# g and h formed with the positions on the partitions, g's statistics as plain sums, and the next pair's squarings beside the first batch's entry

## The chip, the cores and the metric

The kernel runs on one core of a Trainium2 chip, in float32 throughout except for packed sign weights. The metric is device microseconds of one execution. A core has TensorE (PE, matrix products into PSUM), VectorE (DVE), ScalarE (ACT), GpSimd (POOL) and SyncE (SP, which here only issues DMAs); each runs its own queue, and they wait for one another by semaphores.

## The reference, cut to what matters

Four blocks follow one another on x of 8 x 512 x 32 x 32, that is 8 batches of 512 channels and 1024 positions. The change touches only the first:

```
f = relu(batchnorm(Wf x + bf))        # 64 channels; statistics over all batches and positions
g = relu(batchnorm(Wg x + bg))        # 64 channels, the same
h = Wh x + bh                         # 64 channels
z = f^T g                             # 1024 x 1024 for each batch
z2 = (z / largest singular value of z) applied to h
x = Wv z2 + bv + x
```

The second block normalises x over groups of 16 channels and applies an attention over 1024 positions (wq, wk, wv, wp); the third is an attention of its own; the fourth multiplies the signs of x with the signs of a weight matrix. They are done batch by batch in the main loop.

## The kernel before, in words

**First block without z.** z is never formed. The largest singular value comes from the 64 x 64 Gram matrices f f^T and g g^T (their product has the squared singular values of z as eigenvalues), and h g^T gives what h needs. Two batches make a pair: their 64-channel rows stand side by side on the 128 partitions and in the 128 columns of a Gram product, so there are four pairs.

**First stage** (L1229 to L1274). For each batch, x (four chunks of 128 channels by 1024 positions) is the moving operand and the weights of f, g or h are stationary. Each of f, g and h is a PSUM bank: 64 channels of the first 512 positions on the lower partitions, those of the last 512 on the upper. f and g are copied to SBUF (L1261, L1264) and their statistics taken by BN_STATS (L1262, L1265), channels on the partitions. h is biased (L1269), and in the next batch turned by four TensorE transposes (`turn`, L1131) into a tile with the positions on the partitions, one tile for each pair (`ht_pair`). Loads of x go round two buffers on SP's queue, so the load for batch b waits until batch b - 2 is used up; other weights are loaded behind them. In between come the signs of the last block's weights (b = 3, 5) and, in the last batch ahead of h, the turning of wq (`natural`, L1201).

**Statistics** (L1368 to L1398). The batch statistics are gathered, summed over the two partition halves with a product against `fold`, and made into a scale and a bias for each channel; ScalarE then applies scale, bias and relu to f and g in one instruction per batch (`relu`, L1361) and f is stored to DRAM for later.

**Squarings of the last pair** (L1447 to L1456). `turned_pair` (L1347) turns f and g by eight transposes each and `gram` (L1332) forms a Gram matrix by eight products. `chain` (L1009) multiplies the two Gram matrices and then squares the result 20 times, with a rescaling by its trace at every third one; at the end a logarithm of the traces gives the singular value. The batches 6 and 7 go first (their x is still in SBUF), so the last pair's chain runs in a stretch where TensorE's order is the order of the code (`tc.manual_schedule`); between two squarings stand steps of `filler` (L1418): products of weights with weights, then Gram matrices of the other three pairs (`grams`, L1355), with a relu of another batch at each step. Outside that stretch, and on the other engines everywhere, a planner sets each engine's order by readiness and code order with a cost model.

**Entry of the first batch** (`entering`, L859, `enter`, L401). In the same written order come seven steps: the products of the batch's weights, four visits (one for each 128 channels: products of f with the weights, added into x on VectorE with L420, statistics by L423), and two steps of group statistics. The remaining filler steps stand between them: 2, 3, 3, 3, 3, 4, 6 (L1457).

**Main loop** (`fast`, L878). For each of the eight batches come the two attentions and the last block. The products with seven instead of eight terms (`seven`, L332; products by L387) fill most of it. The chains of the other three pairs (`behind`, L1122) run here: `chore` (L887) makes one squaring at every second step while there are any; a chain has 22 steps, 21 of them with a squaring.

Of the kernel before, what the change touches and what calls it, by code (L numbers as in the profile page):

```python
# [8 lines left out]
F32 = mybir.dt.float32  # L9
F16 = mybir.dt.float16  # L10
I32 = mybir.dt.int32
AF = mybir.ActivationFunctionType
# [73 lines left out]
def kernel(  # L86
# [58 lines left out]
    def side(i):  # L145

        return slice(i * MID, (i + 1) * MID)
# [14 lines left out]
    fg = sbw["fg"] = a1.tile([P, CC, P], F32, tag="fg", name="fg")  # L162
    for cc in range(CC):
        nc.scalar.dma_start(out=fg[:, cc, :], in_=w_fg[:, cc, :])
    first = load_x(0, True)
    load_w("h", w_h, [P, CC, MID], a1, nc.scalar)
# [27 lines left out]
    nc.gpsimd.memset(ones1, 1.0)  # L194

# [5 lines left out]
    bhc = const.tile([P, 1], F32, tag="bhc", name="bhc")  # L201
    wv2 = const.tile([P, C], F32, tag="wv2", name="wv2")
    for i in range(2):
        nc.gpsimd.dma_start(out=bhc[side(i), :], in_=rows[0:MID].rearrange("(p o) -> p o", o=1))
# [922 lines left out]
    fs, gs = ([a1.tile([P, HF], F32, tag=f"{n}{b}", name=f"{n}{b}") for b in range(B)] for n in "fg")  # L1127
    ht_pair = [a1.tile([P, NT, P], F32, tag=f"ht{j}", name=f"ht{j}") for j in range(NPAIR)]
    st = a1.tile([P, 2, B, 6], F32, tag="st", name="st")
# [97 lines left out]
    w0 = [sbw["fg"][:, :, 0:MID], sbw["fg"][:, :, MID:], sbw["h"]]  # L1227
    last = None
    for b in range(B):  # L1229
# [7 lines left out]
        banks = [bank() for _ in w0]  # L1237

        def products(i, cc):
            for h in range(NH):  # L1240
                mm(  # L1241
                    out=banks[i][side(h), :],
                    lhsT=w0[i][:, cc, :],
                    rhs=xt[:, cc, half(h)],
                    start=cc == 0,
                    stop=cc == CC - 1,
                )

        if b == 0:
            for cc in range(CC):  # L1250
                for i in range(2):
                    products(i, cc)
        for i in range(3):
            if b == B - 1 and i == 2:
                for _ in natural("q", "w3"):
                    pass
            if b or i == 2:
                for cc in range(CC):
                    products(i, cc)
            if i == 0:  # L1260
                nc.scalar.copy(fs[b], banks[i])  # L1261
                nc.vector.bn_stats(st[:, 0, b, :], fs[b])  # L1262
            elif i == 1:
                nc.vector.tensor_copy(gs[b], banks[i])  # L1264
                nc.vector.bn_stats(st[:, 1, b, :], gs[b])  # L1265
                if last is not None:
                    turn(last[0], last[1], ht_pair[last[0] // 2], 0)
        hraw = a2.tile([P, HF], F32, tag="hraw", name="hraw")
        nc.scalar.activation(hraw, banks[2], AF.Identity, bias=bhc)  # L1269
        last = b, hraw  # L1270
        if b == 3:
            total3 = sign_weights()
        if b == 5:
            scale_signs(total3)  # L1274

# [71 lines left out]
    def turned_pair(j):  # L1347
        ft = a2.tile([P, NT, P], F32, tag="ft", name="ft")
        gt = a2.tile([P, NT, P], F32, tag="gt", name="gt")
        for src, dst in ((fs, ft), (gs, gt)):  # L1350
            for i in range(2):
                turn(2 * j + i, src[2 * j + i], dst, i)
            yield ft, gt
# [7 lines left out]
    def relu(b, i):  # L1361
        t = (fs, gs)[i][b]
        nc.scalar.activation(t, t, AF.Relu, bias=bi0[:, i : i + 1], scale=sc0[:, i : i + 1])
        if i == 0:
            nc.sync.dma_start(out=f_dram[b], in_=t)


    mv = a1.tile([P, 2, 2], F32, tag="mv", name="mv")  # L1368
    mean = a1.tile([P, 2], F32, tag="mean", name="mean")
    dev = a1.tile([P, 2], F32, tag="dev", name="dev")  # L1370
    for i in range(2):
        nc.vector.bn_aggr(mv[:, i, :], st[:, i, :, :])
    nat_k = natural("k", "q")
    next(nat_k)
    turn(last[0], last[1], ht_pair[last[0] // 2], 0)
    ps = bank()
    mm(out=ps[:, 0:2], lhsT=fold, rhs=mv[:, :, 0], start=True, stop=True)
    nc.vector.tensor_copy(mean, ps[:, 0:2])
    nc.vector.tensor_tensor(dev, mv[:, :, 0], mean, ALU.subtract)
    nc.vector.tensor_tensor(dev, dev, dev, ALU.mult)  # L1380
    nc.vector.tensor_tensor(dev, dev, mv[:, :, 1], ALU.add)
    ps = bank()
    mm(out=ps[:, 0:2], lhsT=fold, rhs=dev, start=True, stop=True)
    sc0 = rsqrt_eps(a1, ps[:, 0:2], 2, "r0")
    bi0 = a1.tile([P, 2], F32, tag="bi0", name="bi0")
    m0 = a1.tile([P, 2], F32, tag="m0", name="m0")
    c0 = COL["L0_conv_bf"]
    bias, gamma, beta = (ct[:, c0 + 2 * i : c0 + 2 * i + 2] for i in range(3))
    nc.vector.tensor_tensor(sc0, sc0, gamma, ALU.mult)
    nc.vector.tensor_tensor(m0, mean, bias, ALU.add)  # L1390
    nc.vector.tensor_tensor(bi0, bias, m0, ALU.subtract)
    nc.vector.tensor_tensor(bi0, bi0, sc0, ALU.mult)
    nc.vector.tensor_tensor(bi0, bi0, beta, ALU.add)
    jl = order[0] // 2
    for i in range(2):
        for k in range(2):
            relu(2 * jl + k, i)
# [49 lines left out]
    relus = iter([(2 * j + k, i) for j in rest for i in range(2) for k in range(2)])  # L1447
    with tc.manual_schedule(engines={mybir.EngineType.PE}):
        steps = entering(0)
        for k, _ in enumerate(chain(jl, True)):  # L1450
# [3 lines left out]
            for args in (next(relus, None),):  # L1454
                if args:
                    relu(*args)  # L1456
        for n in (2, 3, 3, 3, 3, 4, 6):  # L1457
            next(steps)
            for _ in range(n):
                next(todo, None)  # L1460
        for _ in todo:
            pass
# [193 lines left out]
```

## Time and profile before

| | us |
|---|---|
| median of 3 runs | 1911.45 (1911.01 to 1911.63) |
| the profiled execution | 1911.79 |
| its span | 1909.9 |
| PE busy | 1886.4 |
| DVE busy | 1130.2 |
| ACT busy | 510.3 |
| first stage, until the last product of h | 4.6 to 98.1 |
| statistics, first Gram matrices | 98.1 to 114.0 |
| squarings of the last pair | 114.0 to 162.6 |
| entry of the first batch, to the first product on differences | 162.6 to 195.1 |
| main loop | 195.1 to the end |

The profile is of one execution. In a chain of waits each line has a start and a length in us, the engine, the tile written and the line of the code. In lines that list instructions, "x48" is the number of records; a float32 product leaves two records. In windows of busy time each engine's figure is the us in which it worked.

### The profile page before, as it was taken

How to read it: one execution, taken by the hardware profiler on the slowest of the kernel's cores; microseconds unless marked ns; L12 is line 12 of the kernel's file. 1: busy time of each engine (PE TensorE's matmuls, PEld its weight loads, DVE VectorE, ACT ScalarE, POOL GpSimd, SP SyncE). 2: the span in 40 equal slices, each digit the busy share in tenths (PEclk: the TensorE clock that was granted, in tenths of full speed). 3: DMA queues.
4: the chain of work that ended last, by engine and by line, in shares of the span. 5: the costliest groups of instructions: out<-in, count | busy, mean ns of one | idle time of the engine just before them, and what ended most of it. 6: DMA issues, size and time to landing. Idle time of an engine off the chain costs nothing.

```text
span 1909.9 us, 16334 instructions
## 1 busy us (share of the span) xinstructions
PE 1886.4 (99%) x6118; PEld 977.5 (51%) x6118; DVE 1130.2 (59%) x1762; ACT 510.3 (27%) x811; POOL 224.5 (12%) x176
## 2 busy tenths in 40 slices
PE   9999999999999999999999999999999999999997
PEld 4366456544745447444645446544645455544653
DVE  3256676448664677447664676457753775466547
ACT  2142121134212332035202431034202521234014
POOL 0000011201121011200121011201120011101121
PEclk9999999999999999999999999999999999999999
DMA  8420000002000120002000120002000200010001
GB/s 320 159 78 6 0 6 12 1 12 88 17 1 0 34 72 12 1 11 88 17 1 0 38 68 12 0 13 87 11 1 9 91 12 0 1 34 22 12 0 46
DMA packets 27782, 66.45 MB, mean 35 GB/s; under 512 B 4272, under 2 KB 5424, under 8 KB 27056
## 3 DMA queue, kind: packets, MB, share of 16 engines
q1 hardware_dynamic: 26768, 64.90, 10.1%
q8 instruction: 50, 0.82, 0.2%
q10 hardware_dynamic: 864, 0.43, 0.1%
q14 instruction: 36, 0.29, 0.1%
q0 software_dynamic: 64, 0.00, 0.0%
HBM read 38.51 MB, written 18.87 MB: 30 GB/s over the span
## 4 chain that ended last, share of the span: by engine, by line
PE 92%; DVE 7%; issue 1%; ACT 1%; DMA 0%; POOL 0%; DVEq 0%; ACTq 0%
PE bank L387 42%; PE bank L556 20%; PE bank L951 6%; PE bank L805 6%; PE bank L1241 5%; PE bank L657 3%; PE bank L411 2%; PE bank L674 2%; DVE both L748 1%; DVE both L718 1%; PE wide L1281 1%; PE wide L1335 1%; PE bank L1022 1%; PE bank L1023 1%; PE bank L697 1%; PE bank L826 1%
## 5 line engine op out<-in xcount | busy, mean ns | idle before, releaser
L556 PE MATMUL bank<-e,vt 128*128 128x512 f32 x768 | 334.2, 593 | 0.0
L556 PEld LDWEIGHTS bank<-e,vt 128*128 128x128 f32 x768 | 144.9, 190 | 174.8 <-issue 173.2
L387 PE MATMUL bank<-ut,h 128*128 128x512 f32 x384 | 182.3, 597 | 0.0
L344 DVE TENSOR_TENSOR e<-bank,e 128x512 f32<-128x512 f32 x128 | 87.8, 686 | 81.9 <-PE bank L387 80.8
L387 PE MATMUL bank<-us,hs 128*128 128x512 f32 x256 | 121.5, 597 | 1.3 <-DVE us L316 0.5
L387 PEld LDWEIGHTS bank<-ut,h 128*128 128x128 f32 x384 | 71.4, 190 | 95.6 <-issue 84.0
L951 PE MATMUL bank<-e,tpg 128*128 128x512 f32 x256 | 114.7, 595 | 0.0
L805 PE MATMUL bank<-tpg 128*128 128x512 f32 x256 | 114.6, 592 | 0.0
L812 ACT ACTIVATE e<-bank 128x512 f32<-128x512 f32 x128 | 76.4, 597 | 128.6 <-PE bank L805 128.6
L387 PE MATMUL bank<-h,wu 128*128 128x512 f32 x192 | 90.4, 593 | 2.4 <-DVE h L462 1.7
L387 PE MATMUL bank<-wo,h 128*128 128x256 f32 x384 | 91.8, 382 | 0.0
L817 DVE TENSOR_TENSOR esum<-esum,e 128x1024 f32<-128x1024 f32 x48 | 58.8, 1225 | 54.9 <-ACT e L812 54.9
L359 POOL TENSOR_TENSOR e<-e 128x512 f32<-128x512 f32 x32 | 43.4, 1356 | 403.8 <-ACT e L338 238.3
L951 PEld LDWEIGHTS bank<-e,tpg 128*128 128x128 f32 x256 | 48.1, 190 | 63.2 <-issue 63.1
L805 PEld LDWEIGHTS bank<-tpg 128*128 128x128 f32 x256 | 48.6, 190 | 60.7 <-issue 60.5
L387 PEld LDWEIGHTS bank<-wo,h 128*128 128x128 f32 x384 | 71.6, 190 | 13.5 <-ACT vt L338 4.1
L359 POOL TENSOR_TENSOR ut<-ut 128x512 f32<-128x512 f32 x16 | 21.7, 1359 | 476.1 <-ACT ut L340 476.1
L344 DVE TENSOR_TENSOR vt<-bank,vt 128x512 f32<-128x512 f32 x64 | 44.1, 689 | 56.2 <-PE bank L387 55.8
L387 PEld LDWEIGHTS bank<-us,hs 128*128 128x128 f32 x256 | 47.1, 190 | 54.9 <-issue 48.3
L834 DVE RECIPROCAL rsum<-bank 128x512 f32<-128x512 f32 x15 | 50.4, 3358 | 38.2 <-PE bank L826 38.2
L685 ACT ACTIVATE sg<-xt,rb 128x512 f16<-128x512 f32 x64 | 45.0, 718 | 103.7 <-DVE xt L676 100.2
L1241 PE MATMUL bank<-xt,fg 128*64 128x512 f32 x256 | 59.5, 613 | 4.6 <-DMA fg<-in_w_fg 4.6
(330 smaller groups left out, 3017.2 us busy)
## 6 DMA issues: line engine op xcount, KB each, us to landing
xt<-in_x SPq DMA_DIRECT2D x55, 512.0 KB
out<-both SPq DMA_DIRECT2D x63, 256.0 KB
rfull<-rsum SPq DMA_DIRECT2D x60, 128.0 KB
f_dram<-f SPq DMA_DIRECT2D x8, 256.0 KB
fb<-f_dram SPq DMA_DIRECT2D x8, 256.0 KB
w<-in_w SPq DMA_DIRECT2D x1, 1024.0 KB
q<-in_w_q SPq DMA_DIRECT2D x1, 1024.0 KB
k<-in_w_k SPq DMA_DIRECT2D x1, 1024.0 KB
```

The source lines that it names most:

```text
L344: nc.vector.tensor_tensor(dst, ps, u, ALU.add)
L359: nc.gpsimd.tensor_tensor(c22, c22, c12, ALU.add)
L387: mm(out=ps[:, q * w : (q + 1) * w], lhsT=lt(ka, kb, q, k), rhs=rhs(ka, kb, q, k), start=first and q == 0 and k == 0, stop=last and k == 1 ...
L556: mm(out=ps, lhsT=a[:, t, bass.ts(r_, P)], rhs=e[t], start=first and t == 0, stop=last and t == NTH - 1, skip_group_check=True,)
L657: mm(out=ps[:, i, :], lhsT=xt[:, cc, bass.ts(4 * h + i, P)], rhs=sbw["tpg"][:, cc, 2 * P : 3 * P], start=cc == 0, stop=cc == CC - 1,)
L685: nc.scalar.activation(sg[:, cc, :], xt[:, cc, half(h)], AF.Sign, bias=rb3[:, cc : cc + 1])
L805: mm(out=ps, lhsT=pt[:, 0, bass.ts(t, P)], rhs=tt[:, 0, half(h)], start=True, stop=True,)
L812: nc.scalar.activation(e[:, half(h)], ps, AF.Exp, scale=float(P) ** -0.5)
L817: nc.vector.tensor_tensor(esum, esum, e, ALU.add)
L834: nc.vector.reciprocal(r, ps)
L951: mm(out=banks[h], lhsT=gt[:, t, :], rhs=es[t][:, half(h)], start=t == 0, stop=t == NT - 1,)
L1241: mm(out=banks[i][side(h), :], lhsT=w0[i][:, cc, :], rhs=xt[:, cc, half(h)], start=cc == 0, stop=cc == CC - 1,)
```

## The change

f is formed as before, but after g and h. For g and h the roles are exchanged: 128 positions of x are the stationary operand and the 128 columns of both weights together the moving one, 8 groups of positions x 4 chunks for each batch, so both leave PSUM with the positions on the partitions and are written straight into the pairs' tiles. g then needs no transposes, nor h. g's channels are now in the free direction, so its statistics are sums over positions: VectorE adds g and its square over the 8 groups, and a product against 1/(B N) adds over the partitions. From g a pilot is taken off first (the mean of batch 0), so that the variance as a difference of sums stays accurate. Scale and bias of g are rows now: they are spread over the partitions by two products with the identity, and applied by two VectorE operations and a relu for each half of a pair (`relu_g`). In batch 0 the products follow the chunks as they arrive. `natural("q", ...)` comes after the last batch. `turned_pair` turns f alone. In the entry of the first batch, the filler steps become 2, 2, 2, 2, 2, 3, 4 and behind the first three of each stands one step of the next pair's chain, 16 of its 22 in all.

```diff
-    fg = sbw["fg"] = a1.tile([P, CC, P], F32, tag="fg", name="fg")
-    for cc in range(CC):
-        nc.scalar.dma_start(out=fg[:, cc, :], in_=w_fg[:, cc, :])
+    wf = a1.tile([P, CC, MID], F32, tag="wf", name="wf")
+    wgh = a1.tile([P, CC, 2, MID], F32, tag="wgh", name="wgh")
+    for cs in (slice(0, 1), slice(1, CC)):
+        nc.scalar.dma_start(out=wf[:, cs, :], in_=w_fg[:, cs, 0:MID])
+        nc.scalar.dma_start(out=wgh[:, cs, 0, :], in_=w_fg[:, cs, MID:])
+        nc.scalar.dma_start(out=wgh[:, cs, 1, :], in_=w_h[:, cs, :])
     first = load_x(0, True)
-    load_w("h", w_h, [P, CC, MID], a1, nc.scalar)
...
+    mean_of = a1.tile([P, P], F32, tag="mean_of", name="mean_of")
+    nc.gpsimd.memset(mean_of, 1.0 / (B * N))
...
-    for i in range(2):
-        nc.gpsimd.dma_start(out=bhc[side(i), :], in_=rows[0:MID].rearrange("(p o) -> p o", o=1))
+    nc.gpsimd.dma_start(out=bh_row, in_=rows[0:MID].partition_broadcast(P))
...
+    def add_up(b, g, dst):
+        sq = a2.tile([P, NT, MID], F32, tag="sq", name="sq")
+        nc.scalar.activation(sq, g, AF.Square)
+        for i, t in enumerate((g, sq)):
+            nc.vector.tensor_reduce(dst[:, i, :], t.rearrange("p t c -> p c t"), AX.X, ALU.add)
+        if b:
+            nc.vector.tensor_tensor(acc, acc, one, ALU.add)
...
+        psf, psg = bank(), wide().rearrange("p (t i c) -> p t i c", i=2, c=MID)
...
+        def products_gh(t, cc):
+            mm(
+                out=psg[:, t, :, :].rearrange("p i c -> p (i c)"),
+                lhsT=xt[:, cc, bass.ts(t, P)],
+                rhs=wgh[:, cc, :, :].rearrange("p i c -> p (i c)"),
+                start=cc == 0 and t % 4 == 0,
+                stop=cc == CC - 1,
+                skip_group_check=True,
+            )
...
         if b == 0:
             for cc in range(CC):
-                for i in range(2):
-                    products(i, cc)
...
+                products_f(cc)
+                for t in range(NT):
+                    products_gh(t, cc)
+        else:
+            for t in range(NT):
                 for cc in range(CC):
-                    products(i, cc)
...
+                    products_gh(t, cc)
+            for cc in range(CC):
+                products_f(cc)
+        g, h = (t[b // 2][:, :, side(b % 2)] for t in (gt_pair, ht_pair))
+        if b == 0:
+            nc.scalar.copy(g, psg[:, :, 0, :])
+            nc.vector.tensor_reduce(pilot, g.rearrange("p t c -> p c t"), AX.X, ALU.add)
+            ps = bank()
+            mm(out=ps[:, 0:MID], lhsT=mean_of, rhs=pilot, start=True, stop=True)
+            nc.vector.tensor_scalar(pilot, ps[:, 0:MID], float(B), None, ALU.mult)
+            nc.vector.tensor_tensor(g, g, over(pilot), ALU.subtract)
+        else:
+            nc.vector.tensor_tensor(g, psg[:, :, 0, :], over(pilot), ALU.subtract)
+        nc.vector.tensor_tensor(h, psg[:, :, 1, :], over(bh_row), ALU.add)
+        add_up(b, g, one if b else acc)
+        nc.scalar.copy(fs[b], psf)
+        nc.vector.bn_stats(st[:, b, :], fs[b])
...
+    for _ in natural("q", "w3"):
+        pass
...
     def turned_pair(j):
         ft = a2.tile([P, NT, P], F32, tag="ft", name="ft")
-        gt = a2.tile([P, NT, P], F32, tag="gt", name="gt")
-        for src, dst in ((fs, ft), (gs, gt)):
-            for i in range(2):
-                turn(2 * j + i, src[2 * j + i], dst, i)
-            yield ft, gt
+        for i in range(2):
+            turn(2 * j + i, fs[2 * j + i], ft, i)
+        yield ft, gt_pair[j]
...
+    def relu_g(j, i):
+        t = gt_pair[j][:, bass.ts(i, NT // 2), :]
+        for k, op in enumerate((ALU.mult, ALU.add)):
+            row = rows_g[:, k].rearrange("p i c -> p (i c)").unsqueeze(1)
+            nc.vector.tensor_tensor(t, t, row.to_broadcast([P, NT // 2, P]), op)
+        nc.scalar.activation(t, t, AF.Relu)
...
+    cols_g = a1.tile([P, 2, P], F32, tag="cols_g", name="cols_g")
+    rows_g = a1.tile([P, 2, 2, MID], F32, tag="rows_g", name="rows_g")
+    ps = bank()
+    for i, t in enumerate((sc0, bi0)):
+        nc.vector.tensor_copy(cols_g[:, i, :], t[:, 1:2].to_broadcast([P, P]))
+        mm(out=ps[:, side(i)], lhsT=cols_g[:, i, :], rhs=ident[:, 0:MID], start=True, stop=True)
...
-        for n in (2, 3, 3, 3, 3, 4, 6):
+        for n in (2, 2, 2, 2, 2, 3, 4):
             next(steps)
-            for _ in range(n):
+            for i in range(n):
                 next(todo, None)
+                if i < 3:
+                    next(behind)
```

## The prediction

> **What bounds the kernel now.** I read the page first, then the chain of waits in order of time from 0 to 310 us, then stretches of it. The page gives the span and the two engines that matter.
>
> ```profile
> span 1909.9 us, 16334 instructions
> PE 1886.4 (99%) x6118; PEld 977.5 (51%) x6118; DVE 1130.2 (59%) x1762; ACT 510.3 (27%) x811; POOL 224.5 (12%) x176
> ```
>
> TensorE is the bound, so a saving has to be TensorE time, or one of its few waits. Chain, first stage (start us, us, what):
>
> ```profile
> 25.43 10.45 PE bank L1241 x48
> 35.88 0.59 PE quad L1135 x4
> 36.47 10.45 PE bank L1241 x48
> 46.92 0.59 PE quad L1135 x4
> ```
>
> A batch takes 46.92 - 35.88 = 11.04 us, with no wait: 24 products of 64 columns, two column halves at once (each product leaves two records), then four transposes of h. The chain of the squarings:
>
> ```profile
> 138.14 0.89 PE wide L1335 x8
> 139.04 0.22 PE bank L1022 x2
> 139.26 0.22 PE bank L1023 x2
> 139.48 1.79 PE wide L1335 x16
> ```
>
> 128-column products with new weights each time go at 1.79/16 = 0.112 us a record, 0.22 a product. One squaring is two: 0.44 us. Here too TensorE is full (the Gram products are filler). The entry of the first batch:
>
> ```profile
> 173.74 1.06 PE bank L411 x4
> 174.80 2.77 PE wide L1281 x6
> 177.57 1.11 PE bank L411 x4
> 178.68 0.74 DVE xt L420
> 179.45 0.70 DVE st L423
> ...
> 182.41 3.54 PE wide L1281 x8
> ...
> 188.90 3.73 DVE h L462 x8
> 192.63 1.15 DVE hs L326
> 193.80 1.24 DVE hs L327
> 195.08 1.13 PE bank L387 x2
> ```
>
> Up to 178.7 a visit takes 1.06 + 2.77 = 3.83 us of TensorE against some 3.05 of VectorE; then VectorE sets the end, and TensorE waits 3.3 us (1.7, 0.7, 0.9 before L387). In the main loop one VectorE instruction per batch marks the period:
>
> ```profile
> 314.63 1.22 DVE L329 TENSOR_TENSOR hs<-h,hs 128x1024 f32<-128x1024 f32 x1
> 536.88 1.21 DVE L329 TENSOR_TENSOR hs<-h,hs 128x1024 f32<-128x1024 f32 x1
> 757.25 1.22 DVE L329 TENSOR_TENSOR hs<-h,hs 128x1024 f32<-128x1024 f32 x1
> 967.64 1.22 DVE L329 TENSOR_TENSOR hs<-h,hs 128x1024 f32<-128x1024 f32 x1
> 1176.40 1.22 DVE L329 TENSOR_TENSOR hs<-h,hs 128x1024 f32<-128x1024 f32 x1
> ```
>
> Periods 222.3, 220.4, 210.4, 208.8. The first two hold 22 squarings of the other pairs each, the later ones none; against their mean of 209.6, a squaring costs (12.7 + 10.8)/44 = 0.53 us of the main loop.
>
> **The Trainium skill.** "TensorEngine Tiling (Array Packing)", Key Properties: changing the tiling mode drains TensorE. The trace agrees: around the four transposes the two changes cost some 0.2 us (0.59, less three gaps of 0.109 between transposes and one more). "VectorE: DVE Perf Modes", tier table and errata: fp32 two-input operations and reductions run at one element a cycle, (N+151)/0.96 ns, 0.69 us for 512. The trace has 0.68 for L1413 (512) and 0.28 for the reductions of 128 (0.29 by the formula); a 512-element TENSOR_REDUCE it doesn't have, so 0.69 is an estimate, and that the strided view costs no more is my choice (0.69 to 1.4). "TensorE: Matmul & The Clock Gate", Part 1: the first microseconds run at half clock; the trace has weight loads 0.85 us apart up to 9.5 us and 0.43 after.
>
> **The change, part by part.**
>
> *First stage, batches 1 to 7.* Per batch: f by four chunks x 0.87 (four records of 0.2177) = 3.48; g and h by 32 products x 2 records x 0.112 = 7.15; two mode changes 0.2; transposes of h gone. 10.81 (10.8 to 10.9) against 11.04: 7 x 0.23 = **-1.6**. *Batch 0* interleaves both forms per chunk, eight changes instead of none: 3.48 + 7.15 + 0.8 = 11.4 against 10.45: **+1.1** (0.5 to 2; the half clock until 9.5 us costs both alike). The weights become six DMAs on ACT's queue instead of five, in 256-byte pieces; they queue behind nothing but one another, ct one issue (0.45 us) later, and it is needed for nothing early. The pilot's product waits for a copy and a reduction, 0.6 + 0.7; batch 1's products stand ready to cover it. Uncovered it costs 1.7. VectorE per batch: two subtractions/additions, two reductions, bn_stats at 0.69 each and a 0.2 sum, 3.7 us, one Square of 0.6 on ACT: hidden in 10.8 us. x must now be whole at a batch's start; x of the next batch is asked for one batch ahead, and DMA falls nearly idle for some 2 us in most batches (12 GB/s at 28 to 30 us), so hidden; a late x would cost up to 2.6 a batch.
>
> Queues: POOL's gets one broadcast of the bias of h in place of two loads and one memset more, SP's gets nothing new (x and weights are asked for in the same order, the stores of f also), so no load is passed by another; I cost this at nothing.
>
> *Statistics to the first Gram.* The transposition of the last h goes (0.50), natural q follows instead of preceding. Six extra small VectorE operations and two turns through TensorE (1.5 us) come in, but relu of f (1.52 on ACT) covers most of the latter. Before, g's two relus (1.42), transposes (0.66) and the Gram of f precede the Gram of g, 5.98 us after the first relu. Now g takes 1.5 + four VectorE operations x 0.69 + an f eviction 0.69 + the last relu 0.6, some 5.5 us, half of the Gram starting before: **-1.0** (-3 to +1).
>
> *Squarings of the last pair.* The same 38 filler steps run; three g-transposition steps (0.9 us each) become three Gram halves (0.9) drawn forward from the entry: no change on TensorE. VectorE takes 12 extra operations, 8.3 us, less three evictions, 2.1. In 114 to 130 us VectorE is busy 5.93 of 16, so most is hidden; in 130 to 144 it is busy 13.69 of 14, and a pair's four (2.8 us, less 0.7 to 1.4) fall there: **+1.3** (0.3 to 4).
>
> *Entry.* 16 squarings come in: 16 x 0.44 + five trace sums x 0.14 = 7.8; three Gram halves left: -2.7. In order: weights step +0.7; visits 1.06 + 2 x 0.86 + 2 x 0.44 = 3.7, as before; mean step 3 x 0.86 + 3 x 0.44 + 0.14 = 4.0 against 3.54, +0.5; last step inside TensorE's old 3.3 us of waiting. TensorE's order is written out, so a squaring holds up everything behind it until the one before is evicted. By ACT that takes 0.37 plus handing over, 0.65, under the 0.86 of filler: no stall. Every third squaring goes through sum, reciprocal and scaling on VectorE: 1.25 us in the main loop (product's end to eviction). There are five. VectorE's queue is in order, and a visit's own 3.05 us may stand ahead. Stalls: weights step 0.5, second visit 0.4 to 1.9 (take 1.1), third 0 to 1 (0.5), mean step 0.5; last step 0 to 1.5 of VectorE's path (0.7). Sum 0.7 + 0.5 + 3.3 = **+4.5** (+2 to +9).
>
> *Main loop.* 16 of 63 squarings leave: 16 x 0.53 = **-8.5** (7.0 by TensorE's bare time, to 9). Without TensorE being full there it would be nothing, but it is busy 209.28 of 209.40 us.
>
> Sum: -1.6 + 1.1 - 1.0 + 1.3 + 4.5 - 8.5 = -4.2. The profiled execution took 1911.79 (span 1909.9 and 1.9 around it), 0.3 above the median of 1911.45. So 1907.6 on its own time, **1907.3** against the median.
>
> **Rivals.** (a) *The squarings are only moved.* TensorE was full in the entry up to 178.7, so the 7.8 us come back whole, with somewhat larger stalls: entry +6.5, sum -2.2, 1909.3. For it: written order. Against it: 3.3 us of waits at the end.
> (b) *The entry hides them.* VectorE slips the small operations between a visit's instructions: stalls gone, entry +1.5, sum -7.2, 1904.3. For it: 0.7 us of VectorE free per visit before; against it: three dependent operations in a row.
> (c) *Slower.* VectorE runs a visit's 3.05 us ahead of every sum-and-scale: each of the five then stalls TensorE 3.05 + 1.25 - 0.86 = 3.4 us, 17 instead of my 3.3 (1.1 + 0.5 + 0.5 + 0.5 + 0.7): +9.5, 1921. It ends slower by 0.2% once the five average over (3.3 + 8.0)/5 = 2.3 us. Against it: only two or three fall inside a visit.
>
> **Chances.** 0.2%, about what a measurement of this kernel can tell from no change, is 3.8 us: below 1907.6 is faster. Forecast (-2.5 to -6.5) 0.52, of which 0.35 beyond -3.8; (a) (-2.5 to +2) 0.20; (b) (-6.5 and below) 0.16; (c) and its milder forms (above +2) 0.12, 0.10 of it beyond +3.8. Faster 0.51, same 0.39, slower 0.10. Range 1902.5 to 1913.5: it leaves out the worst of (c) and the best of (b) and reaches the ends of the entry's cost. The forecast's own: 1905 to 1909.
>
> **What would show it.** In the chain of the changed kernel: batches 1 to 7 some 10.8 us apart and batch 0 ending about 1 us later than before; the first squaring of the last pair 1 to 2 us before 114.0; from it to the first product on the differences (195.1) some 86 us where there were 81.0, with waits of TensorE for squarings' evictions of about 3 us in the entry; the first period marked by L329 still some 222, with its 22 squarings, and the second about 212 instead of 220.4, since only some 6 squarings are left for it. I would be wrong if those waits pass 6 us in all, if batch 0 or the pilot leaves TensorE idle for over 2 us, if a batch waits for x, or if the main loop gives back less than 7 us.

## The result, and the profile after

The changed kernel takes 1920.56 us (median of 5 runs, 1919.56 to 1921.56) against 1911.01 (5 runs, 1910.23 to 1911.63): a ratio of 1.0051, interval 1.004 to 1.0062. It is slower by 0.5%. I had predicted 1907.3, and my range ended at 1913.5, so both the time and its sign were wrong. The profiled execution took 1919.56 us, 1.0 below this median, and the one of before 0.8 above its own: the profiles differ by 7.8 us where the medians differ by 9.55.

The page after, first two lines:

```profile
span 1917.7 us, 16784 instructions
PE 1886.4 (98%) x6320; PEld 1007.7 (53%) x6320; DVE 1152.1 (60%) x1796; ACT 507.1 (26%) x808; POOL 224.4 (12%) x176
```

TensorE is busy for the same 1886.4 us as before, so the 7.8 us of longer span are time in which TensorE stands still: 31.3 us instead of 23.5. That is the balance of the whole execution; stage by stage its work moves too, out of the main loop and into the entry.

The timeline of TensorE in the changed kernel (start us, us, line, operands, count, and in brackets the wait ahead of it), first stage:

```profile
4.20 2.52 PE L1262 MATMUL bank<-xt,wf 128*64 128x512 f32 x4 [4.20 <-DMA wf<-in_w_fg]
7.43 3.75 PE L1271 MATMUL wide<-wgh,xt 128*128 128x128 f32 x16 [0.70 <-DMA wgh<-in_w_h]
...
27.96 3.65 PE L1262 MATMUL bank<-xt,wf 128*64 128x512 f32 x16
31.55 7.41 PE L1271 MATMUL wide<-wgh,xt 128*128 128x128 f32 x64
38.89 3.65 PE L1262 MATMUL bank<-xt,wf 128*64 128x512 f32 x16
...
111.27 2.05 PE L1371 MATMUL wide<-ft 128*128 128x128 f32 x16 [1.14 <-ACT ft L1151]
116.31 0.49 PE L1026 MATMUL bank<-gm 128*128 128x128 f32 x2 [0.56 <-DVE gm L1380]
...
118.00 0.35 PE L1058 MATMUL bank<-tj,mask 128*128 128x1 f32 x2 [0.98 <-DVE tj L1054]
```

A batch takes 38.89 - 27.96 = 10.93 us (11.04 before). Batch 0 first waits 0.70 us for the weights of h, and its 16 records of g and h take 3.75 us at the low clock (the clock records give full speed from 11.12 us on), where the next 16 take 2.05. The first squaring starts at 116.31, where it was at 114.03.

The same view, entry of the first batch. L415 are the products of a visit, L1317 filler, L1026 and L1058 a squaring and its trace, L391 the first product of the main loop:

```profile
174.88 1.13 PE L415 MATMUL bank<-fb,pv 64*128 64x512 f32 x4
...
177.49 1.10 PE L1317 MATMUL wide<-p,nat_v 128*128 128x512 f32 x2
179.60 0.49 PE L1026 MATMUL bank<-cur 128*128 128x128 f32 x2 [1.01 <-DVE cur L1048]
180.24 1.13 PE L415 MATMUL bank<-fb,pv 64*128 64x512 f32 x4
...
184.83 0.38 PE L1058 MATMUL bank<-tj,mask 128*128 128x1 f32 x2 [0.65 <-DVE tj L1054]
185.14 1.13 PE L415 MATMUL bank<-fb,pv 64*128 64x512 f32 x4
...
201.97 1.98 PE L391 MATMUL bank<-h,wu 128*128 128x512 f32 x4 [0.81 <-DVE h L466]
```

The four visits start 3.87, 5.36 and 4.90 us apart; before it was 3.90, 3.83 and 3.83. A squaring waits 1.01 us for its rescaled operand. The main loop's first product, at 189.58 before, starts at 201.97.

VectorE in the main loop, the instruction that marks the periods (L333 now, L329 before):

```profile
208.55 1.22 DVE L333 TENSOR_TENSOR hs<-h,hs 128x1024 f32<-128x1024 f32 x1
328.42 1.22 DVE L333 TENSOR_TENSOR hs<-h,hs 128x1024 f32<-128x1024 f32 x1
550.93 1.22 DVE L333 TENSOR_TENSOR hs<-h,hs 128x1024 f32<-128x1024 f32 x1
765.56 1.22 DVE L333 TENSOR_TENSOR hs<-h,hs 128x1024 f32<-128x1024 f32 x1
975.58 1.22 DVE L333 TENSOR_TENSOR hs<-h,hs 128x1024 f32<-128x1024 f32 x1
```

The periods are 119.9, 222.5, 214.6 and 210.0 us, with 18, 22, 7 and no squarings. Before they were 118.6, 222.2, 220.4 and 210.4, with 19, 22, 22 and none. So the third period gained 5.8 us and the first lost 1.3.

Cut at marks that both traces have, the 7.8 us of span lie as follows (us; "to the main loop" runs from the last of the 21 squarings to the first L333 or L329):

| stretch | predicted | measured | where it is read |
|---|---|---|---|
| the eight batches | -0.5 | +1.7 | start of what follows their products, 96.3 (98.05 without the 1.75 of wq) to 98.0 |
| from there to the first squaring, wq counted in both | -1.0 | +0.6 | 17.7 to 18.3 |
| chain of the last pair | +1.3 | +1.3 | 42.28 to 43.55 |
| entry, to the main loop | +4.5 | +8.9 | 39.78 to 48.69 |
| main loop to the end | -8.5 | -4.7 | 1713.86 to 1709.19 |
| sum | -4.2 | +7.8 | |

Two rows carry 8.2 of the 12.0 us between prediction and result: the entry and the main loop, the two ends of the 16 moved squarings.

### The profile page after: what moved, and what is told of

The parts are those of the page before. It is cut to its first block, busy times and chain, and to the rows that moved or that the text cites. A ratio compares the mean times of both kernels' runs of the same rounds, so it can differ in the third digit from the quotient of the medians.

```text
span 1917.7 us, 16784 instructions
## 1 busy us (share of the span) xinstructions
PE 1886.4 (98%) x6320; PEld 1007.7 (53%) x6320; DVE 1152.1 (60%) x1796; ACT 507.1 (26%) x808; POOL 224.4 (12%) x176
## 4 chain that ended last, share of the span: by engine, by line
PE 59%; DVE 4%; issue 0%; ACT 0%; DVEq 0%; ACTq 0%
PE bank L391 29%; PE bank L560 15%; PE bank L955 4%; PE bank L809 4%; PE bank L661 2%; PE bank L678 1%; PE bank L415 1%; DVE both L722 1%; DVE both L752 1%; PE bank L701 1%; PE bank L830 1%; DVE xt L680 0%; DVE both L714 0%; DVE us L320 0%; DVE us L317 0%
## 5 line engine op out<-in xcount | busy, mean ns | idle before, releaser
L391 PE MATMUL bank<-ut,h 128*128 128x512 f32 x384 | 182.4, 597 | 0.7 <-ACT e L353 0.7
L391 PE MATMUL bank<-us,hs 128*128 128x512 f32 x256 | 121.5, 597 | 1.3 <-DVE us L320 0.5
L391 PEld LDWEIGHTS bank<-ut,h 128*128 128x128 f32 x384 | 71.4, 190 | 96.7 <-issue 85.2
L391 PE MATMUL bank<-wo,h 128*128 128x256 f32 x384 | 91.9, 382 | 0.0
L391 PE MATMUL bank<-h,wu 128*128 128x512 f32 x192 | 90.5, 593 | 1.5 <-DVE h L466 0.8
L391 PEld LDWEIGHTS bank<-wo,h 128*128 128x128 f32 x384 | 71.7, 190 | 14.3 <-ACT vt L342 4.9
L391 PEld LDWEIGHTS bank<-us,hs 128*128 128x128 f32 x256 | 47.3, 190 | 56.4 <-issue 49.5
L1271 PEld LDWEIGHTS wide<-wgh,xt 128*128 128x128 f32 x512 | 59.6, 196 | 8.8 <-issue 8.8
```

Source lines behind the costliest of these rows:

```text
L391: mm(out=ps[:, q * w : (q + 1) * w], lhsT=lt(ka, kb, q, k), rhs=rhs(ka, kb, q, k), start=first and q == 0 and k == 0, stop=last and k == 1 ...
L1271: mm(out=psg[:, t, :, :].rearrange("p i c -> p (i c)"), lhsT=xt[:, cc, bass.ts(t, P)], rhs=wgh[:, cc, :, :].rearrange("p i c -> p (i c)"), ...
```

## The experiments

**The two halves of the change.** Theory A says that the squarings carry the loss; its rival says that the new form of g and h does. The first run leaves the squarings where they were, in the changed kernel:

```diff
             for i in range(n):
                 next(todo, None)
-                if i < 3:
-                    next(behind)
```

> The changed kernel without the squarings in the entry (filler steps 2, 2, 2, 2, 2, 3, 4 kept, all 63 squarings of the other pairs back in the main loop). Theory A (the squarings written into the entry are what made it slower): last squaring of the last pair to first VectorE instruction L333 on the differences falls from 48.7 us to 36 to 38 (before: 39.8), because three Gram halves less are left there; main loop back from 1709.1 to about 1714; total 1910 to 1912.5. Theory B (the new form of g and h, by its batches, statistics and VectorE work, carries the loss): total 1916 or more.

Measured: 1912.65 us, ratio 1.0007 (0.9998 to 1.0016). The second puts the same 16 squarings into the kernel before:

```diff
-        for n in (2, 3, 3, 3, 3, 4, 6):
+        for n, m in ((2, 2), (3, 2), (3, 2), (3, 2), (3, 2), (4, 3), (6, 3)):
             next(steps)
-            for _ in range(n):
+            for i in range(n):
                 next(todo, None)
+                if i < m:
+                    next(behind)
```

> The kernel before, with 16 squarings of the next pair in the entry (2 in each of the first five steps, 3 in each of the last two; filler steps 2, 3, 3, 3, 3, 4, 6 as before). Theory A: entry from 39.8 us to about 50, main loop 5 to 8 us shorter, total 1914 to 1918. Theory B: the squarings pay for themselves, total 1904 to 1910.

Measured: 1918.51 us, ratio 1.0035 (1.0021 to 1.005), a little above what A expected. The entry grew to 50.7 as expected, but the main loop fell by 3.8 us only, where A had 5 to 8. In this profile the clock records show half speed for 3.4 us from 200.5 on, inside the entry, which is some 1.7 us of it (an estimate: half of the stretch). Both runs say A: without the squarings the changed kernel is close to the one before, and the squarings cost 7.9 us on the changed kernel and 7.6 on the one before, or about 6 if the clock stretch is taken off.

The first run also splits the ledger. It has the first squaring at 116.80, the chain at 43.55, the entry at 35.90 and the main loop at 1713.82. So without the squarings the change makes the entry *shorter* by 3.9 us, which pays for what it loses earlier. Two things do that together: three Gram halves are gone from the entry, and the visits have two filler steps instead of three. Near the end of this section the spacing is changed by itself in the kernel before. Against that run, the 16 squarings add 12.8 us to the entry and take 4.6 from the main loop. Two windows of the entry, without and with the squarings (first the run without; columns: window, its length, busy time and instructions of each engine):

```profile
160.35:196.25 35.90, 32.36 (x123) 15.57 (x122) 26.19 (x65) 7.63 (x11) 1.02 (x1) 1.00 0.03 8
```

The changed kernel:

```profile
159.86:208.55 48.69, 42.25 (x196) 24.31 (x195) 32.51 (x93) 11.62 (x22) 1.56 (x2) 1.00 0.02 6
```

TensorE's busy time rises by 9.9 us (I had counted 7.8) and its idle time by 2.9, from 3.5 to 6.4. The idle time of the first run, in its list of TensorE's waits (total us, times, longest), has as its largest part a wait for VectorE, and none for h:

```profile
PE bank L436 <- DVE mv L435: 1.5, 1, 1.5
```

**The last step: what holds up h.** In the changed kernel, h (L466) starts 6.6 us after the products on the differences, where 2.8 were usual. VectorE's timeline there:

```profile
197.56 0.15 DVE L449 TENSOR_TENSOR bi<-ct,bi 128x4 f32<-128x4 f32 x1
197.68 0.55 DVE L1048 TENSOR_SCALAR cur<-bank,r 128x256 f32<-128x256 f32 x1
200.73 0.29 DVE L1053 TENSOR_TENSOR diag<-cur,ident 128x128 f32<-128x128 f32 x1 [2.51 <-ACT cur L1040]
201.06 0.29 DVE L1054 TENSOR_REDUCE tj<-diag 128x1 f32<-128x128 f32 x1
201.32 0.17 DVE L1539 MEMSET ones<- 128x128 f32 x1
201.40 3.71 DVE L466 TENSOR_SCALAR h<-xt,r_r,bi 128x512 f32<-128x512 f32 x8
```

The bias of h is ready at 197.7. VectorE's queue then holds the trace of the 16th squaring (L1053), which waits 2.51 us for a squaring that TensorE has not yet made, and h stands behind it. This is theory Q: the queue delays h. Theory M says that h itself waits until TensorE is through with the last filler products. The test takes one squaring out of the last step, the one whose trace stands ahead of h:

```diff
-        for n in (2, 2, 2, 2, 2, 3, 4):
+        for n, m in ((2, 2), (2, 2), (2, 2), (2, 2), (2, 2), (3, 3), (4, 2)):
...
-                if i < 3:
+                if i < m:
```

> The changed kernel with two squarings instead of three in the last step of the entry, so that the 16th, the one whose trace is prepared on VectorE (L1053, L1054), is back in the main loop. Theory Q (that trace stood ahead of the normalisation of h in VectorE's queue and held it back): h (L466) starts when its own scale and bias are ready, about 198.3 instead of 201.4; total about 1918. Theory M (h waits for TensorE to finish the last filler products, whose tiles it takes over): h starts about 200.8; total 1920.

Measured: 1916.15 us, ratio 1.0029 (1.0017 to 1.004). VectorE with 15 squarings:

```profile
197.67 0.15 DVE L449 TENSOR_TENSOR bi<-ct,bi 128x4 f32<-128x4 f32 x1
197.79 0.55 DVE L1048 TENSOR_SCALAR cur<-bank,r 128x256 f32<-128x256 f32 x1
198.31 0.17 DVE L1539 MEMSET ones<- 128x128 f32 x1
198.39 3.61 DVE L466 TENSOR_SCALAR h<-xt,r_r,bi 128x512 f32<-128x512 f32 x8
```

And its TensorE:

```profile
198.94 1.88 PE L1317 MATMUL wide<-p,nat_v 128*128 128x512 f32 x4
200.66 1.88 PE L391 MATMUL bank<-h,wu 128*128 128x512 f32 x4
```

h starts 3.0 us earlier, while TensorE's filler runs on to 200.66, so M falls and Q is right on what held h. The main loop's products start 1.3 us earlier only: they now run on from the filler without a wait, so TensorE's own work in the last step sets their start. The entry falls from 48.69 to 45.46. The total fell 2 us below the 1918 that Q had expected. The main loop has one squaring more to do and still becomes shorter, 1708.21 against 1709.19, since a wait of 1.2 us in its first period is gone (below). So one squaring, placed last, costs 4.4 us by the medians, nearly half of the whole loss; this counts its own products in the entry together with its place in the queue.

**Statistics to the first squaring.** From the first relu of f to the first squaring the trace has 105.64 to 114.03 before, 105.59 to 116.31 after: 10.7 us instead of 8.4. VectorE works there on g of the other pairs (L1403), so I moved those to GpSimd:

```diff
-            nc.vector.tensor_tensor(t, t, row.to_broadcast([P, NT // 2, P]), op)
+            eng = nc.vector if j == order[0] // 2 else nc.gpsimd
+            eng.tensor_tensor(t, t, row.to_broadcast([P, NT // 2, P]), op)
```

> The changed kernel with the two operations of relu_g for the three other pairs on GpSimd instead of VectorE (12 instructions, those of the last pair stay). Theory D (relu_g of pairs not yet needed filled VectorE's queue ahead of the first Gram matrices and the first squarings): first squaring at 114.5 to 115.2 instead of 116.3, its trace no longer waited for, total about 1918. Rival (the delay comes from ScalarE's relus and the turning of f): first squaring within 0.5 us of 116.3, total within 1 us of 1920.6.

Measured: 1925.09 us, ratio 1.0076 (1.0059 to 1.0092), slower still. VectorE, changed kernel, the four operations on the pair that is waited for:

```profile
106.74 2.50 DVE L1403 TENSOR_TENSOR gt<-gt,rows_g 128x512 f32<-128x512 f32 x4
```

The same four with GpSimd at work beside them:

```profile
105.05 5.73 DVE L1404 TENSOR_TENSOR gt<-gt,rows_g 128x512 f32<-128x512 f32 x4
```

Each takes 1.43 us instead of 0.62, and TensorE then waits 4.05 us where it waited 1.14:

```profile
112.48 2.63 PE L1371 MATMUL wide<-ft 128*128 128x128 f32 x16 [4.05 <-ACT ft L1151]
```

The Trainium skill, "SBUF — State Buffer", Who interferes with whom, says that a VectorE instruction with two SBUF inputs contends with a GpSimd instruction that reads SBUF; this run agrees. The stretch from the end of the batches grew from 18.3 to 22.4 us. Not all of that is the edit: in this profile the clock records show half speed for 3.4 us from 113.8 on, and the two Gram products under it took 2.63 (above) and 2.85 us, where the changed kernel has 2.05 for each:

```profile
115.50 2.85 PE L1371 MATMUL wide<-gt 128*128 128x128 f32 x16 [0.38 <-DVE gm L1380]
```

Without these 1.4 us it is 21.0, and the wait of 4.05 us ended before the half speed began. So moving the work lost more than it was to free.

Theory D puts the delay down to VectorE taking these operations ahead of what the last pair needs. The order of the code is kept for them:

```diff
-            nc.vector.tensor_tensor(t, t, row.to_broadcast([P, NT // 2, P]), op)
+            did = nc.vector.tensor_tensor(t, t, row.to_broadcast([P, NT // 2, P]), op)
+            if j != order[0] // 2 and k == 0:
+                tc.keep_in_program_order(did)
```

> The changed kernel with relu_g of the three other pairs pinned behind what the code has put on VectorE before it, so that it can't be drawn ahead of the first Gram matrices. Theory D (VectorE's queue was full of it): 98.0 to first squaring falls from 18.3 us to 16.5 to 17.3, and the 20 squarings take 42.3 to 44 us; total 1918.5 to 1920. Rival (the longer path of g's scale and bias, or of the turning of f): 18.3 stays within 0.5.

Measured: 1919.75 us, ratio 1.0041 (1.0026 to 1.0057). From the end of the batches to the first squaring it takes 18.2 us, against 18.3, and the chain becomes 0.7 longer. TensorE's wait of 0.98 us for the first trace is gone, but the rest of the chain grows by more. D falls.

**Batch 0.** It alternates the two forms of product chunk by chunk; is that what it loses, or is it the clock? The edit writes all of f first:

```diff
         if b == 0:
             for cc in range(CC):
                 products_f(cc)
+            for cc in range(CC):
                 for t in range(NT):
                     products_gh(t, cc)
```

> The changed kernel with all of f's products of batch 0 ahead of those of g and h, so that one change of the tiling mode is left of eight, and the weights of g and h are not needed until f is done. Theory F (mode changes and the wait for the weights of h lengthened batch 0): the first product after the eight batches (wq turned, 98.0 us) comes 1 to 1.5 us earlier at the same time of the full clock, total about 1919.3. Rival (the late full clock alone): the time follows the full clock by half a microsecond for each microsecond and is otherwise unchanged, 97.5 to 98.3.

Measured: 1920.17 us, ratio 1.0045 (1.0029 to 1.006), and the batches end at 98.1, as in the changed kernel. But TensorE's timeline of this run still has the two forms in turns, since the planner reorders them there; the number of changes of form hardly fell, and the run does not decide on them. What the profiles do show is the clock. In the ten with the new first stage, the clock records give full speed from anywhere between 8.0 and 14.1 us (11.12 in that of the changed kernel), and in the eight of them that leave batch 7 as it is, the batches end at 92.4 + half of that moment, within 0.3 us: from 96.30 where it is 7.97 to 98.84 where it is 13.10. So half of 11.12 - 9.78, 0.7 us, of the first row's 1.7 goes with the clock. Whether it belongs to the execution or to the kernel stays open: the four profiles with the old first stage have the moment at 9.1 to 9.8 (9.78 in that of before), so the wide spread, and on the average a later moment, came with the new stage. All ten have a wait of 0.3 to 1.4 us for the weights of h behind the first four records, which the old stage has not; no run took it away, and its length does not order the moments.

**What can be mended.** The changed kernel without squarings and with both small edits (f first in batch 0, the code's order for g):

```diff
-        for n in (2, 2, 2, 2, 2, 3, 4):
+        for n, m in zip((2, 2, 2, 2, 2, 3, 4), (0, 0, 0, 0, 0, 0, 0)):
...
-                if i < 3:
+                if i < m:
```

> The changed kernel with no squarings in the entry, relu_g in order, and f first in batch 0. If the three mended places add up: 1912.65 less 1.2 (batch 0) less 1.3 (relu_g) = 1910.2, 1909 to 1911.5, within 0.1% of the kernel before. If they don't, 1912 to 1913.5.

Measured: 1912.43 us, ratio 1.0003 (0.9994 to 1.0011): as without the edits. Then three squarings, put where TensorE waits (one in the first step, two in the last visit's):

```diff
-        for n, m in zip((2, 2, 2, 2, 2, 3, 4), (0, 0, 0, 0, 0, 0, 0)):
+        for n, m in zip((2, 2, 2, 2, 2, 3, 4), (1, 0, 0, 0, 2, 0, 0)):
```

> As e7_gh_mended, with three squarings in the entry: the first in the weights step, where VectorE stands idle, and two evicted by ScalarE ahead of the group statistics, where TensorE waits 1.5 us for VectorE. If such waits hide squarings: entry 0 to 1 us longer than in e7_gh_mended, main loop 1.5 us shorter, total 0.5 to 1.5 us below it. If the written order costs even there: entry 1.5 us longer or more, total the same or above.

Measured: 1911.46 us, ratio 1.0 (0.9991 to 1.0008). The entry grows by 0.67 us, all of it in the first step (3.01 to 3.68), and the main loop shrinks by 1.4. So the two squarings beside the wait of 1.5 us cost nothing there, while the one in the first step costs what it gives back.

Theory N: the turning of wq after the last batch delays the statistics. Here it stands between g, h and f of the last batch:

```diff
+            if b == B - 1:
+                for _ in natural("q", "w3"):
+                    pass
...
-    for _ in natural("q", "w3"):
-        pass
-
```

> As e8_three_squarings, with the turning of wq back inside the last batch, between the products of g and h and those of f, as it stood ahead of h's products in the kernel before. Theory N (the turnings of wq, wk and wv one behind another, on two PSUM tiles and beside the statistics, are what the way to the first squaring lost): start of the turning of wq plus f's products to first squaring falls by 1 to 2 us against e8_three_squarings (there 98.2 without the late clock to first squaring: 18.2), total 1909.5 to 1910.7. Rival (the longer path of g's scale and the turning of f): same to 0.3 us.

Measured: 1913.43 us, ratio 1.0013 (1.0006 to 1.002). Less half of the moment of full clock, the first squaring comes at 111.7 us (118.23 - 13.01/2), where the two runs without this edit have 110.4 and 110.7. N falls: wq was cover for the statistics of f, which now start later (their first product, by the same reckoning, at 97.1 us, where the run with three squarings has 94.4). A fourth squaring, in the last step, on top:

```diff
-        for n, m in zip((2, 2, 2, 2, 2, 3, 4), (1, 0, 0, 0, 2, 0, 0)):
+        for n, m in zip((2, 2, 2, 2, 2, 3, 4), (1, 0, 0, 0, 2, 0, 1)):
```

> As e9_q_inside, with a fourth squaring in the entry, in the last step, evicted by ScalarE and followed by the products for its trace on VectorE while that waits for GpSimd. If it hides there: entry within 0.3 us of e9_q_inside, main loop 0.5 us shorter, total 0.3 to 0.5 us less. If its trace holds h back as the 16th squaring did: entry 0.6 to 3 us longer.

Measured: 1912.98 us, ratio 1.0009 (1.0003 to 1.0016). Entry +0.3, main loop -0.4: nothing won.

**A version that beats both.** If the entry gained in the first run because a visit with two filler steps suits VectorE better than one with three, the kernel before should gain by that alone, the freed steps falling to its wait for h:

```diff
-        for n in (2, 3, 3, 3, 3, 4, 6):
+        for n in (2, 2, 2, 2, 2, 4, 6):
```

> The kernel before with the filler steps of the entry at 2, 2, 2, 2, 2, 4, 6 in place of 2, 3, 3, 3, 3, 4, 6, so that the four moved ones run in the last step, beside VectorE's own path. If VectorE needs no more than two fillers in a visit (as in e1_gh_only, three visit periods in 8.9 us instead of 11.6) and the last step hides the rest: entry 36 to 37.5 us instead of 39.8, total 1907.5 to 1909.5. If the fillers then end after h and hold back the first products on it by as much as the visits gained: total within 1 us of 1911.

Measured: 1908.97 us, ratio 0.999 (0.9983 to 0.9997); entry 37.19 instead of 39.78, main loop 1714.00. So the spacing alone, without the change, gains 2.6 us in the entry and 2.1 in all. Held against the first run of this section, which has nearly this spacing and no squarings but the new form of g and h, it is 3.7 us faster (1908.97 to 1912.65): the new form looked like no change only because the better spacing came with it. With the three squarings that cost little:

```diff
-        for n in (2, 2, 2, 2, 2, 4, 6):
+        for n, m in zip((2, 2, 2, 2, 2, 4, 6), (1, 0, 0, 0, 2, 0, 0)):
             next(steps)
-            for _ in range(n):
+            for i in range(n):
                 next(todo, None)
+                if i < m:
+                    next(behind)
```

> As e11_before_2_fillers, with three squarings of the next pair in the entry, at the places of e8_three_squarings. If these places hide them here too: entry 0.7 us longer than in e11_before_2_fillers, main loop 1.4 us shorter, total 0.5 to 1 us less. If not: total the same or more.

Measured: 1908.08 us, ratio 0.9983 (0.9976 to 0.999), below both kernels; entry 37.85, main loop 1712.43. TensorE's wait for the statistics, 1.5 us with the two fillers alone, is 0.6 here:

```profile
PE bank L432 <- DVE mv L431: 0.6, 1, 0.6
```

Two of its 19 executions took 2479.16 and 5156.37 us, all others 1907.2 to 1908.5 (the ratio is without these two); what happened in these two stays open, and it would have to be known before this version is used.

## Why the prediction was wrong

**The step that failed** is the entry's "last step inside TensorE's old 3.3 us of waiting", with its 0.7 us for VectorE's path. From the product on the differences to h it grew by 3.8 us. Two things were wrong in it.

The room was not there. The 3.3 us were three waits, and only the first stands ahead of the main loop's first product; the others stand behind it, and the changed kernel still has them. Before, then after:

```profile
189.58 1.96 PE L387 MATMUL bank<-h,wu 128*128 128x512 f32 x4 [1.70 <-DVE h L462]
192.21 1.98 PE L387 MATMUL bank<-h,wu 128*128 128x512 f32 x4 [0.68 <-ACT ut L349]
195.08 1.98 PE L387 MATMUL bank<-hs,su 128*128 128x512 f32 x4 [0.88 <-DVE hs L327]
...
204.63 1.98 PE L391 MATMUL bank<-h,wu 128*128 128x512 f32 x4 [0.67 <-ACT ut L353]
207.65 1.96 PE L391 MATMUL bank<-hs,su 128*128 128x512 f32 x4 [1.04 <-DVE hs L331]
```

And the 1.7 us were spent without any squaring. Of the 6 filler steps written for the old last step only 2 were left when it came; the new one has 4. In the run without squarings these already end where h is ready, and nothing is waited for:

```profile
186.03 3.68 PE L1317 MATMUL wide<-p,nat_v 128*128 128x512 f32 x8
189.75 1.96 PE L391 MATMUL bank<-h,wu 128*128 128x512 f32 x4
```

The second error is VectorE's queue, in which each third squaring puts two operations and where h stands behind whatever comes first. I had named the pattern for the visits ("VectorE's queue is in order, and a visit's own 3.05 us may stand ahead") and only in that direction: the squaring behind the visit. At the end of the entry it is the other way round, the batch's own critical instruction behind a squaring's trace. The run with 15 squarings shows it: h then starts 3.8 us after the product on the differences, 0.7 more than before, as the prediction had it, and the whole kernel is 4.4 us faster.

**The entry's other terms.** Weights step +0.7 and 0.5: measured +1.6 (3.32 to 4.96), short by 0.4. Visits 1.1 and 0.5: measured +2.6 over the three periods (11.56 to 14.13), short by 1.0. The waits were right there (1.01 and 0.65 us); TensorE's work was not, for which I had put nothing ("3.7, as before") and which rose by 0.9 (from 11.56 to 12.46 us busy). Mean step +0.5 of work and +0.5 of waiting: measured +1.0, but all of it work (3.76 to 4.73 us busy), so that this sum is right by luck. Over the entry TensorE works 7.1 us more (35.1 to 42.2), where I had counted 7.8 - 2.7 = 5.1, and its idle time grows by 1.8 instead of taking work in. The run without squarings has visits of 2.97 us, so the squarings really added 14.13 - 8.92 = 5.2 us over three: a third filler step in a visit could be had elsewhere at less cost, and the comparison with the old visit hid that. VectorE did slip the small operations between a visit's instructions, as rival (b) has it, but the first two each wait behind an operation of 0.7 us:

```profile
177.43 0.73 DVE L424 SCALAR_TENSOR_TENSOR xt<-bank,bvo,xt 128x512 f32<-128x512 f32 x1
178.08 0.15 DVE L1059 COPY tr<-bank 128x1 f32<-128x1 f32 x1
178.20 0.69 DVE L427 BATCH_NORM_STATS2 st<-xt 128x6 f32<-128x512 f32 x1
178.81 0.15 DVE L1081 RECIPROCAL r<-tr 128x1 f32<-128x1 f32 x1
178.93 0.21 DVE L429 BATCH_NORM_AGGREGATE mv<-st 128x2 f32<-128x12 f32 x1
179.06 0.49 DVE L1048 TENSOR_SCALAR cur<-bank,r 128x256 f32<-128x256 f32 x1
```

Three short operations, 0.79 us in all, end 1.9 us after TensorE's sum (177.62); the 1.01 us that TensorE waits for the last is the difference less one filler step.

**The main loop, -8.5.** Measured -4.7. "16 x 0.53" took the mean price of a squaring and applied it at the margin. In the third period, which 15 squarings left, TensorE's busy time fell by 7.1 us (220.25 to 213.15), 0.47 each: the price was a little high. And the period fell by 5.8 only, because waits of the seven-term products came up that the squarings had covered. TensorE's waits in the third period of the changed kernel:

```profile
PE bank L391 <- ACT e L353: 0.7, 1, 0.7
PE bank L391 <- DVE e L348: 0.7, 1, 0.7
```

Before, TensorE was idle for 0.12 us in that period, and 1.5 now (both from windows of it). And the first period, with one squaring less, has a wait that it didn't have:

```profile
PE bank L1026 <- DVE cur L1046: 1.2, 1, 1.2
```

With 15 squarings the first period is back at 118.8 us. I had argued that TensorE "is busy 209.28 of 209.40 us" in a later period; that shows a period without squarings is full too, not that the same order without them leaves no gap. That the main loop would give back less than 7 us was one of my signs of being wrong, and it came. The three squarings of the smaller version give back 0.5 each, the 16 together 0.29.

**The first stage.** Batches 1 to 7, -1.6: a batch takes 10.93 and not 10.81; 7 x 0.11 gives -0.8. The records of g and h follow one another at 0.112 us as predicted, and those of f as before; the two changes of form cost 0.3 us (7.34 - 7.15 and 3.59 - 3.48), for which I had put 0.2. Batch 0, +1.1: what is left of the measured 1.7 is +2.5, of which about 0.7 is the later clock (I had written that it "costs both alike") and 0.7 the wait for the weights of h, which I had costed at nothing ("they queue behind nothing but one another"): they do, and of each part of the weights h's come last. The bound that I gave for this batch, 0.5 to 2, holds without the clock.

**Statistics to the first Gram, -1.0**, measured +0.6, inside the range that I gave (-3 to +1). The way to the first relu became shorter, and the 2.3 us from there to the first squaring are the loss. I had put half of the Gram product ahead of g's last steps. In the trace the Gram of f itself starts late, at 111.27 instead of 109.12. Two things are seen ahead of it. The second f's relu ends at 107.11, but its transposes stand behind 2.74 us of filler in TensorE's order and start at 109.20. Then 1.14 us of TensorE wait for the copy of turned f on ScalarE, where before the transposes of g ran. The second is there without the first too: with wq inside the last batch no filler stands between the transposes, and the wait is 1.16. No run moved the filler or the relus of f alone, so what each costs stays open.

**What was right**: the second period at 222 and the squarings left for the third (7, I said some 6). The chain of the last pair is +1.3 as counted, but only the size: I had put it where VectorE is full, at 130 to 144 us, and 0.98 of it is the wait for the first trace, at 118.00, behind g of the other pairs. TensorE's waits on the squarings in the entry add up to 3.0 us, as predicted ("about 3"), and below the 6 that I named as the sign of being wrong: these waits were not what I had to watch.

**The rivals.** (c) gave 1921, and the result is 1920.56, but not by its mechanism: it asks for stalls of TensorE of over 2.3 us on average at five rescalings, and the longest is 1.0. (b)'s mechanism was seen, without its gain. (a), that the squarings are only moved, comes nearest in kind: the first run against the changed kernel says that they cost 12.8 us where they went and free 4.6 where they were. I gave 0.10 to slower, on the assumption that the loss could only come from stalls of TensorE at the rescalings, and left the main loop's return out of every rival.

## What to carry to other kernels

Before moving work into a stretch where one engine waits, follow the queue of every engine that the work touches, and ask what stands behind each new instruction; count as room only the waits that stand ahead of the first thing you hold up. A small operation that waits ahead of the critical one costs its whole wait. Price the stretch that the work leaves at the margin, not at the mean: part of it was covering waits, and these come back. And try the piece that makes the new room by itself: here fewer fillers in a visit, with nothing else changed, gained 2.1 us, where the change lost 9.55.

## What the runs showed of the hardware

A VectorE addition with two operands in SBUF, 0.62 us for 128x512, took 1.43 us while GpSimd ran the same kind of operation. A reduction over a strided view of 512 elements took 1.04 us where my estimate was 0.69 (the mean of seven in the changed kernel's first stage, where TensorE does not wait for it). Full clock began between 8.0 and 14.1 us in ten profiles with nearly the same first stage (9.1 to 9.8 in four with the old one), and the end of the batches followed by half of it, from 96.30 to 98.84 us in eight of the ten. In two profiles the clock fell to half for 3.4 us later on, at 200.5 and at 113.8 us. A difference of 2 us between two single profiles says little until these records are compared.
